# Layer 1 of a gated recurrence: when GpSimd adds x, and where VectorE's additions of sums stand

## The chip, the cores and the metric

The kernel runs on one core of a Trainium2 chip, in one launch. The time is device microseconds of that core. TensorE does the matrix products into PSUM banks, ScalarE (ACT) the sigmoids, tanhs and copies into PSUM, VectorE (DVE) and GpSimd (POOL) the elementwise work, SyncE (SP) starts the transfers. Each engine takes its instructions in the program's order and waits on semaphores for the others. In the profile PEld is TensorE's loading of weights, which runs beside its products.

## The reference

Two recurrent layers of width 512 over 64 sequences of 128 steps, with a residual after each, all in float32:

```python
x = x + L0(x, cond)          # gates by sigmoid, normalised; cumulative products and sums over time
vz, vr, vh = cond @ C_z + b_z, cond @ C_r + b_r, cond @ C + b
xz, xr, xh = x @ W_z, x @ W_r, x @ W
def step(h, (xzt, xrt, xht)):
    z  = sigmoid(xzt + h @ U_z + vz)
    r  = sigmoid(xrt + h @ U_r + vr)
    hh = tanh(xht + (r * h) @ U + vh)
    h  = (1 - z) * h + z * hh
    return h, h
out = x + scan(step, 0, ...)
```

Layer 1 (the `step` above) is a chain of 128 steps: h of a step is needed for the gates of the next.

## The kernel before

Layer 0 runs until about 690 us, in 16 groups of 4 sequences. It is not touched.

Layer 1 splits the 64 sequences into two streams of 32. A step of one stream follows a step of the other, so that one stream's elementwise work can run under the other's products. In the text a *half step* is one step of one stream, about 4.5 us from its first sigmoid to the next one's (of the other stream); two make the step of all sequences. In the code, `halves` makes it in two parts, with a `yield` between them.

What a half step issues, with its lines:

- TensorE: the products of h with U_r and U_z (`g<-w_s,h`, L464), then one or two products for later steps, then those of r*h with U (`g<-w_s,fi`, L464), then again one or two products for later steps (L602).
- ScalarE: r (L918), z (L927), tanh (L957), and copies of the share of x and cond of a coming step into the gates' bank (`put_share`, L871).
- VectorE: r*h (L922) and its transpose (L923), each in two halves of 64 columns; in the second part z*hh (L969), the new h (L970) and its transpose (L974).
- GpSimd: 1-z (L933) and (1-z)*h (L934).
- The output: GpSimd adds x to the transposed h (L985, into `hh`), VectorE transposes that back into the output tile (L994), and SP stores four steps at a time (L1028). The call of L994 waits in a list, `deferred`, and is made in the first part of the next half step, after the reads.

The products for later steps are x @ W of all three gates for 8 steps of all sequences at once. They are made by two nested levels of a scheme with 7 products instead of 8 (classes and functions `Outer`, `products`, `sum_tasks`, `place`). It needs sums of blocks of x before the products (GpSimd, L810, drawn by `take_sums`) and sums of blocks of the result after them. For the latter the program keeps lists:

- `to_read`: results in PSUM banks. `read(n)` takes up to n of them: VectorE adds a result to a block in SBUF (`W<-r,W`, L704), for some of them first a common part (L699). A bank can be written again only when it has been read; `free` reads on until it has. So the position of a read on VectorE sets when a product (or a copy by ScalarE, L615) that uses the bank again can start.
- `to_add_c`: additions of two SBUF blocks on VectorE (`W<-W`, L719); `add_c()` takes one. `to_add`: the same on GpSimd (L724).
- `to_store`: finished blocks, stored by SP to DRAM (L732) at the start of the next half step; a step loads its share from there (L865).

In a half step of the program before, the order of the calls around the change is: in the first part, r*h (L922, L923), z, L933 and L934, shared parts, `add(1)` (L724), `take_sums` (L810), products, `read(reads[0] and ...)`, `deferred` (L994); in the second part the products of r*h, tanh, L969, L970, L974, then L985, `add_c()` (L719) and `read(reads[1])`. `reads` is (4, 1) or (4, 0) for most steps and (2, 2) where a stream takes two steps in a row. The last 7 steps of each stream (`apart`, from step 121) split the gates differently and have no L985.

The order on each engine is pinned as the program issues it (`pin`); transfers are placed around it.

Of the kernel before, what the change touches and what calls it, by code (L numbers as in the profile page):

```python
# [12 lines left out]
ALU = mybir.AluOpType  # L13
# [6 lines left out]
def kernel(  # L20
# [38 lines left out]
    nc = tc.nc  # L59
# [11 lines left out]
    SB = B // 2  # L71
# [7 lines left out]
    def pin(instruction):  # L79
        return tc.keep_in_program_order(instruction)  # L80
# [199 lines left out]
    def chunk_products(g, c, between=None):  # L280

        f, i = fs[c % 2], is_[c % 2]
        fb, ib = by_batch(f), by_batch(i)
        p = gate(g, c, 0)
        pin(nc.scalar.activation(fb, p, AF.Sigmoid, bias=biasT[:, 0, c : c + 1]))
        if g == 0 and c == 0:
            w0_transposed(0, 2)
        elif g == 0 and c + 1 < K:
            w0_transposed(c + 1, 0)
        if between:  # L290
            between()
        p = gate(g, c, 1)
        pin(nc.scalar.activation(ib, p, AF.Sigmoid, bias=biasT[:, 0, K + c : K + c + 1]))
        if g == 0 and c == 0:
            transposed(condT, cond_sb, n=B)
            w0_transposed(1, 0)
        elif g == 0 and c + 1 < K:
            w0_transposed(c + 1, 1)
        if g + 1 < NG:
            for u, m in ((), ((0, 0), (0, 1)), ((1, 0),), ((1, 1),))[c]:  # L300
                x_joined(g + 1, u, m)
        p = gate(g, c, 2)
        if g == 0 and c + 1 < K:
            for n in range(1 if c == 0 else 2, 3):
                w0_transposed(c + 1, n)
        return p
# [135 lines left out]
    def conditioning():  # L442

        vs = []
        for s in range(2):
            p = psum.tile([P, 3, P], F32, tag="tp", name=f"pv{s}")
            matmuls(p, lambda k: condT[:, k, s * SB : (s + 1) * SB], [cw[:, k] for k in range(K)])
            whole = const.tile([P, 3, P], F32, name=f"whole_v{s}")
            pin(nc.vector.tensor_tensor(whole, p, bias1, ALU.add))
            vs.append(whole)  # L450
        return vs
# [106 lines left out]
    def x_of(st, t):  # L558

        return x4[t // TH][:, :, t % TH, st.batches]  # L560
# [4 lines left out]
    class Outer:  # L565
# [121 lines left out]
        def read(self, block, common):  # L687


            (m, j), n, r = block, self.n, self.bank(block)  # L690

            while n in (0, 5) and (m, j) in waiting:
                add(1)
            while n == 5 and (m, j) in waiting_c:
                add_c()
            if j == 1 and not common:
                if not hasattr(self, "common"):
                    shared_to_copy[0]()
                pin(nc.vector.tensor_tensor(r, r, self.common, ALU.add))  # L699
                return  # L700
            u, s5, c = (acc[:, i, m, j] for i in range(3))
            v1, v21 = v_x[:, j], v_x[:, 2 + j]
            dst, other = ((u, v1), (c, u), (u, u), (s5, v21), (c, s5), (u, u), (c, u))[n]
            pin(nc.vector.tensor_tensor(dst, r, other, ALU.add))  # L704
            unread.discard(r.name)
            if n == 1:
                self.store(c, 0, m, j)
            elif n == 4:
                waiting_c.add((m, j))
                to_add_c.append(lambda: self.add_c(c, u, m, j))  # L710
            elif n == 5:
                waiting.add((m, j))
                to_add.append(lambda: self.add(s5, u, m, j))
            elif n == 6:
                self.store(c, 1, m, j)

        def add_c(self, c, u, m, j):
            waiting_c.remove((m, j))
            pin(nc.vector.tensor_tensor(c, c, u, ALU.add))  # L719
            self.store(c, 0, m, 2 + j)  # L720

        def add(self, s5, u, m, j):
            waiting.remove((m, j))
            pin(nc.gpsimd.tensor_tensor(s5, s5, u, ALU.add))  # L724
            self.store(s5, 1, m, 2 + j)
# [13 lines left out]
    to_copy, shared_to_copy = [], []  # L739
    to_read, unread = [], set()  # L740
    to_add, waiting = [], set()
    to_add_c, waiting_c = [], set()
# [10 lines left out]
    sums_to_take, taken = [], set()  # L753
# [12 lines left out]
    def sum_tasks(group):  # L766
# [24 lines left out]
        def halves(d):  # L791
            *ts, op = d
            return [(*[t[:, k] for t in ts], op) for k in range(HC)]

        outer = [
            [(base - 1, ("s", group, i, k), d_) for k, d_ in enumerate(halves(d))]
            for i, d in enumerate(wsums(x_[0][0], x_[0][1], x_[1][0], x_[1][1], s_))
        ]
# [6 lines left out]
    def take_sums(n):  # L805
        for m in range(n):
            if not sums_to_take or sums_to_take[0][0] > state["begun"]:
                return m
            _, name, a = sums_to_take.pop(0)
            pin(nc.gpsimd.tensor_tensor(*a))  # L810
            taken.add(name)
        return n

    ahead = []
# [21 lines left out]
    class Stream:  # L836
# [56 lines left out]
        def halves(self, t, filler=None, between=None, targets=lambda: (0, 0), busy=False, reads=(4, 0)):  # L893
# [40 lines left out]
                    pin(nc.gpsimd.tensor_tensor(r, r, h_, ALU.mult))  # L934
            while shared_to_copy:
                shared_to_copy[0]()
            add(1)
            take_sums(2 if busy else 3)
            place(targets()[0], busy)
            if filler:  # L940
                filler()
            read(reads[0] and max(reads[0], len(to_read) - 2))
            while deferred:
                deferred.pop(0)()
            if between:
# [3 lines left out]
            h, hT, hh = (tile_[:, n] for n in range(3))  # L949
# [31 lines left out]
            if apart:  # L981
                deferred.append(output)
                return
            pin(
                nc.gpsimd.tensor_tensor(  # L985
                    hh.rearrange("p (k b) -> p k b", b=SB),
                    hT.rearrange("p (k b) -> p k b", b=SB),
                    x_of(self, t),
                    ALU.add,
                )  # L990
            )

            def output():
                pin(nc.vector.transpose(o, hh))  # L994
                self.store(t)

            deferred.append(output)
            if APART <= t + AHEAD < S:

                pin(nc.gpsimd.tensor_copy(ident.rearrange("p (k b) -> p k b", b=SB), x_of(self, t + AHEAD)))  # L1000
                deferred.append(lambda: pin(nc.vector.transpose(self.output(t + AHEAD), ident)))
            add_c()
            read(reads[1])
            if t + 2 < S and not direct(self, t + 2) and all((t + 2, q) in stored for q in range(Q)):
                self.load_share(t + 2)
# [29 lines left out]
    APART, AHEAD = 121, 10  # L1035
    last_outputs = []
    deferred = []
    pending = []

    shares_d = [dram.tile([TW * B, Q, 3 * P], F32, name=f"shares{n}") for n in range(4)]  # L1040

    for g in range(NG):
        for c in range(K):
# [7 lines left out]
            if (g, c) == (1, 1):  # L1051
                vs = []
                p = chunk_products(g, c, between=lambda: vs.extend(conditioning()))
            else:
                p = chunk_products(g, c)
# [160 lines left out]
    for n in range(2):  # L1216
        t = work.tile([P, 5, 3, P], F32, tag="xt", bufs=2, name=f"w_inner{n}")
# [97 lines left out]
        n += len(steps)  # L1315
    while deferred:
        deferred.pop(0)()
    assert not ahead and not to_read and not to_copy and not shared_to_copy and not sums_to_take


# [32 lines left out]
```

## Time and profile before

| | |
|---|---|
| median of 3 runs | 1877.04 us (1876.59 to 1879.87) |
| the profiled execution | 1878.12 us, of which the span of its instructions is 1876.3 |
| mean clock granted to TensorE | 0.999 |
| from 785 to 1800 us: busy PE, PEld, DVE, ACT, POOL | 1014.25, 641.39, 770.97, 455.05, 587.34 of 1015.00 us |
| L922 (r*h) there | 438 times, mean 224 ns |
| L985 (adds x) there | 219 times, mean 497 ns; idle before it 194.6 us, 173.9 of them until L974 |
| L719 there | 53 times, mean 552 ns |
| L810 (sums before the products), 128x128 and 128x256 | 479 to 529 ns, 749 to 792 ns |
| L704 and L699 (reads) there | 539 to 543 ns, 555 ns |

The page names an engine's share of the span, then the chain of work that ended last, followed back from the end. In the timeline each row has a start in us from the span's start, a duration, the engine, the line, output and inputs, and in brackets how long the engine was idle and what ended it. The ends of matmuls are modelled, so the distance from one start to the next tells more of TensorE than the durations.

### The profile page before, as it was taken

Reading aid. Unit: us, or ns where it says so; the run is one execution under the profiler, and the core shown is the slowest. Engines: PE = TensorE matmul, PEld = TensorE weight load, DVE = VectorE, ACT = ScalarE, POOL = GpSimd, SP = SyncE. Lnnn points to the kernel's source line nnn. Section 1 sums busy time; section 2 is a strip of 40 time slices with the busy share of each in tenths; the row PEclk is TensorE's granted clock in tenths of the full one; section 3 lists DMA queues with packets and bytes.
Section 4 is the critical chain, followed back from the end, with each engine's and each line's share of the span. In section 5 each row is a group of like instructions: output and inputs, shape, how many; then the busy total and the mean of one; then the engine's idle time right before and its main releaser. Section 6 shows DMA issues by size and latency. Waiting matters only on the chain.

```text
span 1876.3 us, 62311 instructions
## 1 busy us (share of the span) xinstructions
PE 1864.2 (99%) x24793; PEld 1054.2 (56%) x24793; DVE 1504.9 (80%) x3438; ACT 722.6 (39%) x1888; POOL 865.1 (46%) x1544
## 2 busy tenths in 40 slices
PE   9999999999999999999999999999999999999998
PEld 5444444444444445566666666666666666666567
DVE  5899999999999976777777777777777777777786
ACT  3232223222232233344444444444444444444434
POOL 1233232333333344546556556466565565565650
PEclk9999999999999999999999999999999999999999
DMA  7765433444333241334334344344343343443343
GB/s 181 176 124 119 82 70 73 88 82 83 73 76 65 49 86 29 101 90 142 112 101 142 94 115 133 104 124 126 96 137 109 99 141 101 114 130 96 111 111 78
DMA packets 366754, 195.38 MB, mean 104 GB/s; under 512 B 225332, under 2 KB 352064, under 8 KB 366464
## 3 DMA queue, kind: packets, MB, share of 16 engines
q1 hardware_dynamic: 366280, 191.33, 40.9%
q8 instruction: 195, 3.19, 0.7%
q14 instruction: 95, 0.78, 0.1%
q10 hardware_dynamic: 184, 0.07, 0.0%
HBM read 78.63 MB, written 81.13 MB: 85 GB/s over the span
## 4 chain that ended last, share of the span: by engine, by line
PE 98%; DVE 1%; issue 0%; DMA 0%; ACT 0%; SPq 0%; DVEq 0%; ACTq 0%
PE g L464 36%; PE p L232 35%; PE r L602 14%; PE r12a L602 4%; PE shared L602 4%; PE r12b L602 4%; PE gz L464 1%; PE tp L190 0%; PE pv L464 0%; DMA x<-in_x_dram 0%; DVE W L704 0%; PE g_first L464 0%; DVE fi L923 0%; DVE fi L922 0%; DVE r L339 0%
## 5 line engine op out<-in xcount | busy, mean ns | idle before, releaser
L232 PE MATMUL p<-xT,W 128*128 128x512 f32 (+1 forms) x1560 | 661.9, 586 | 0.0
L232 PEld LDWEIGHTS p<-xT,W 128*128 128x128 f32 x1560 | 293.5, 190 | 361.6 <-issue 359.1
L464 PE MATMUL g<-w_s,h 128*32 128x256 f32 (+1 forms) x8128 | 481.0, 373 | 2.3 <-issue 1.6
L464 PEld LDWEIGHTS g<-w_s,h 128*32 128x32 f32 x8128 | 301.4, 110 | 179.4 <-issue 83.2
L464 PEld LDWEIGHTS g<-w_s,fi 128*32 128x32 f32 x8128 | 222.7, 109 | 113.9 <-issue 55.4
L464 PE MATMUL g<-w_s,fi 128*32 128x128 f32 x8128 | 276.3, 273 | 2.7 <-DVE fi L922 1.3
L922 DVE TENSOR_TENSOR fi<-fi,h 128x64 f32<-128x64 f32 (+1 forms) x494 | 112.3, 227 | 179.3 <-ACT fi L918 178.5
L985 POOL TENSOR_TENSOR h<-h,x 128x128 f32<-128x128 f32 x242 | 121.3, 501 | 232.4 <-DVE h L974 206.8
L314 POOL COPY first<-condT 128x4 f32<-128x4 f32 x64 | 12.6, 196 | 461.8 <-DVE h L386 432.8
L918 ACT ACTIVATE fi<-g 128x128 f32<-128x128 f32 x254 | 70.6, 278 | 327.7 <-PE g L464 308.9
L933 POOL TENSOR_SCALAR fi<-fi 128x128 f32<-128x128 f32 x240 | 72.6, 302 | 236.6 <-DVE fi L922 226.5
L704 DVE TENSOR_TENSOR W<-r,W 128x384 f32<-128x384 f32 x315 | 169.2, 539 | 7.4
L310 ACT ACTIVATE fi<-fi 128x512 f32<-128x512 f32 x64 | 40.4, 631 | 340.6 <-DVE fi L351 340.6
L957 ACT ACTIVATE h<-g 128x128 f32<-128x128 f32 x255 | 70.9, 278 | 236.2 <-PE g L464 236.2
L923 DVE STREAM_TRANSPOSE fi<-fi 128x64 f32<-128x64 f32 (+1 forms) x494 | 122.2, 247 | 22.8 <-PE r12a L602 0.5
L969 DVE TENSOR_TENSOR h<-h,fi 128x128 f32<-128x128 f32 (+1 forms) x264 | 94.9, 359 | 43.8 <-ACT h L957 43.1
L253 POOL TENSOR_TENSOR x<-xT,h 128x512 f32<-128x512 f32 x63 | 122.6, 1946 | 4.9
L934 POOL TENSOR_TENSOR fi<-fi,h 128x128 f32<-128x128 f32 x240 | 110.8, 462 | 20.0
L970 DVE TENSOR_TENSOR h<-h,fi 128x128 f32<-128x128 f32 (+1 forms) x264 | 97.7, 370 | 27.2 <-POOL held L810 0.9
L810 POOL TENSOR_TENSOR held<-held 128x128 f32<-128x128 f32 x240 | 113.7, 488 | 3.1
L602 PE MATMUL r<-w_inner,held 128*32 128x384 f32 x1080 | 114.6, 486 | 0.0
L339 DVE RECIPROCAL r<-r 128x256 f32<-128x256 f32 x60 | 104.2, 1737 | 0.0
(158 smaller groups left out, 2721.5 us busy)
## 6 DMA issues: line engine op xcount, KB each, us to landing
shares<-W SPq DMA_DIRECT2D x240, 192.0 KB, 2.1
xz<-shares SPq DMA_DIRECT2D x480, 48.0 KB, 1.9
whole_v<-shares SPq DMA_DIRECT2D x480, 48.0 KB, 2.0
x2d<-x SPq DMA_DIRECT2D x63, 256.0 KB, 4.2
words<-held SPq DMA_DIRECT2D x240, 64.0 KB, 2.1
out_dram<-o SPq DMA_DIRECT2D x240, 64.0 KB, 1.8
xw_None<-x2d SPq DMA_DIRECT2D x56, 256.0 KB, 3.4
w_rows<-in_L_cond_W_f_dram SPq DMA_DIRECT2D x4, 256.0 KB, 5.7
```

The costliest lines, as they stand in the source:

```text
L232: nc.tensor.matmul(p[:, tokens], lhsT=W0[:, c, n, k, :], rhs=xT[g][:, k, tokens], start=(k == 0), stop=(k == K - 1),)
L253: nc.gpsimd.tensor_tensor(x2.rearrange("p (t b) -> p t b", b=GB)[:, ts], xT[g][:, c, :].rearrange(f"{layout(g)} -> p t b", b=GB)[:, ts], b ...
L339: pin(nc.vector.reciprocal(r, r))
L464: nc.tensor.matmul(p[q * SB : (q + 1) * SB], lhsT=lhsT(k), rhs=part(wk, q), start=(start and k == 0), stop=(stop and k == len(w) - 1), ski ...
L602: nc.tensor.matmul(self.bank(bank)[q * SB : (q + 1) * SB], lhsT=a[:, q * SB : (q + 1) * SB], rhs=w_, start=start, stop=True, skip_group_ch ...
L704: pin(nc.vector.tensor_tensor(dst, r, other, ALU.add))
L810: pin(nc.gpsimd.tensor_tensor(*a))
L922: pin(nc.vector.tensor_tensor(rh[:, e], r[:, e], h_[:, e], ALU.mult))
L923: pin(nc.vector.transpose(rhT[:, e], rh[:, e]))
L934: pin(nc.gpsimd.tensor_tensor(r, r, h_, ALU.mult))
L970: pin(nc.vector.tensor_tensor(h[:, e], hh[:, e], r[:, e], ALU.add))
L985: nc.gpsimd.tensor_tensor(hh.rearrange("p (k b) -> p k b", b=SB), hT.rearrange("p (k b) -> p k b", b=SB), x_of(self, t), ALU.add,)
```

## The change

The addition of x (L985) is no longer issued at the end of a half step's second part. It goes to a new list, `unsummed`, which the first part of the next half step empties: after that step's L933 and L934, and before `add(1)` and the sums. The output's transpose is put into `deferred` at that point, so it still comes in the same first part as before, behind the reads. `add_c()` is no longer called at the end of the second part; it is called in the first part, ahead of the reads, and when it has something to add, the number of reads to take is less by one (unless more than that are waiting beyond two).

```diff
@@ in halves, first part
             while shared_to_copy:
                 shared_to_copy[0]()
+            while unsummed:
+                unsummed.pop(0)()
             add(1)
             take_sums(2 if busy else 3)
             place(targets()[0], busy)
             if filler:
                 filler()
-            read(reads[0] and max(reads[0], len(to_read) - 2))
+            added = len(to_add_c[:1])
+            add_c()
+            read(reads[0] and max(reads[0] - added, len(to_read) - 2))
             while deferred:
                 deferred.pop(0)()
@@ in halves, second part
-            pin(
-                nc.gpsimd.tensor_tensor(
-                    hh.rearrange("p (k b) -> p k b", b=SB),
-                    hT.rearrange("p (k b) -> p k b", b=SB),
-                    x_of(self, t),
-                    ALU.add,
-                )
-            )
 
             def output():
                 pin(nc.vector.transpose(o, hh))
                 self.store(t)
 
-            deferred.append(output)
+            def summed():
+                pin(
+                    nc.gpsimd.tensor_tensor(
+                        hh.rearrange("p (k b) -> p k b", b=SB),
+                        hT.rearrange("p (k b) -> p k b", b=SB),
+                        x_of(self, t),
+                        ALU.add,
+                    )
+                )
+                deferred.append(output)
+
+            unsummed.append(summed)
             if APART <= t + AHEAD < S:
 
                 pin(nc.gpsimd.tensor_copy(ident.rearrange("p (k b) -> p k b", b=SB), x_of(self, t + AHEAD)))
                 deferred.append(lambda: pin(nc.vector.transpose(self.output(t + AHEAD), ident)))
-            add_c()
             read(reads[1])
```

What is computed stays the same.

More of the change, by code (lines that the diff above doesn't have):

```diff
@@ L1037 @@
     deferred = []
+    unsummed = []
     pending = []
@@ L1317 @@
         deferred.pop(0)()
-    assert not ahead and not to_read and not to_copy and not shared_to_copy and not sums_to_take
+    assert not ahead and not to_read and not to_copy and not shared_to_copy and not sums_to_take and not unsummed
 _INS = [
```

## The prediction

> **What bounds the kernel now.** I read the page (busy times, chain of waits), then the timeline of layer 1 half step by half step, then the order of the instructions before and after. The page first:
>
> ```profile
> span 1876.3 us, 62311 instructions
> PE 1864.2 (99%) x24793; PEld 1054.2 (56%) x24793; DVE 1504.9 (80%) x3438; ACT 722.6 (39%) x1888; POOL 865.1 (46%) x1544
> PE 98%; DVE 1%; issue 0%; DMA 0%; ACT 0%; SPq 0%; DVEq 0%; ACTq 0%
> ```
>
> TensorE is full, and the chain that ended last lies on it for 98%. The change adds and removes no matmul, so it can only move what makes TensorE wait in layer 1 (from about 690 us). The busy rows do not show those waits, because the matmuls' ends are modelled; I read them from the starts. Undisturbed, in the timeline around 1404 us, the two products before `fi` start at 1403.85 and 1404.49, `fi` at 1405.14: 0.645 us each. At 1155 us:
>
> ```profile
> 1154.46 0.84 PE L602 MATMUL r<-w_x,x 128*32 128x384 f32 x8
> 1154.47 0.31 DVE L974 STREAM_TRANSPOSE h<-h 128x128 f32<-128x128 f32 x1
> 1154.72 0.28 ACT L918 ACTIVATE fi<-g 128x128 f32<-128x128 f32 x1 [1.58 <-PE g L464]
> 1155.00 0.45 POOL L985 TENSOR_TENSOR h<-h,x 128x128 f32<-128x128 f32 x1
> 1155.03 0.50 DVE L922 TENSOR_TENSOR fi<-fi,h 128x64 f32<-128x64 f32 x1 [0.24 <-ACT fi L918]
> 1155.11 0.84 PE L602 MATMUL shared<-w_inner,held 128*32 128x384 f32 x8
> 1155.57 0.24 DVE L923 STREAM_TRANSPOSE fi<-fi 128x64 f32<-128x64 f32 x1
> 1155.73 0.18 DVE L922 TENSOR_TENSOR fi<-fi,h 128x64 f32<-128x64 f32 x1
> 1155.96 1.08 PE L464 MATMUL g<-w_s,fi 128*32 128x128 f32 x32
> ```
>
> The last product starts at 1155.11, `fi` at 1155.96: 0.85 instead of 0.645, 0.20 us lost. L985 on GpSimd covers 1155.00 to 1155.45; L922, 0.18 to 0.23 elsewhere, takes 0.50 and ends 0.08 after L985. So L922 stands still while L985 runs, and r*h reaches TensorE late. I went through all starts from 785 to 1800 us this way. All losses together are 8.1 us; those over 0.06 us fall into five kinds:
>
> - A: L985 alone lies over L922: 19 places, 2.63 us.
> - B: L969 and L970 stood behind GpSimd's sums L810, so L974 is late, then L922 (as at 863.35): 9 places, 1.89.
> - C: L719 stands at the end of the half step, then L985 comes over L922: 4 places, 0.86 (and 0.40 and 0.21 after 1800).
> - D: a product waits for a read (L704) of its bank: 2 places of 0.46 (1142.99 and 1563.65).
> - E: one of 0.28 at 1415, where the second L923 starts late.
>
> What L719 costs in the middle of a half step is also there, at 920 us:
>
> ```profile
> 919.94 0.46 POOL L934 TENSOR_TENSOR fi<-fi,h 128x128 f32<-128x128 f32 x1
> 920.12 0.70 DVE L719 TENSOR_TENSOR W<-W 128x384 f32<-128x384 f32 x1
> 920.36 0.77 POOL L810 TENSOR_TENSOR held<-x,held 128x128 f32<-128x128 f32 x1
> ```
>
> L719 (0.52 alone) waits for L934's end at 920.40 and ends 0.42 later, at 920.82; the L810 behind it takes 0.77 instead of 0.46 and ends 0.31 after L719. A VectorE addition of two SBUF tiles and a GpSimd operation take turns; reads from PSUM (L704, L699: 0.52 to 0.56) and transposes are not held up.
>
> **The change part by part.** Times below run from the start of a half step's first sigmoid (L918). Undisturbed: L922 at 0.31, last L923 done at 1.20, GpSimd's L933 1.08 to 1.38, L934 1.47 to 1.93, then a slot each 0.42; the next sigmoid at 4.54 (4.47 in some). A late L922 costs TensorE its lateness less about 0.06: 0.27 late cost 0.20, 0.19 cost 0.11.
>
> *L985 behind L934.* 242 additions of 0.46 us move from just after L974 (from 3.6 to 4.5) to 1.88 to 2.34. There VectorE mostly does reads, which do not collide, and no matmul waits for an output. So kind A goes: -2.63. The transpose L994 now waits for L985's end at 2.34. With two reads or more in front VectorE isn't there earlier (1.20+2x0.5); with one read it waits 0.7 us, and L969 behind it starts at 2.6 rather than at tanh's end, 2.4: 0.2 us on a chain whose result TensorE needs a step of the other stream later. Cost 0. The output's copy to DRAM goes later by at most this; nothing waits for it.
>
> *The sums L810 one slot later.* L985 takes the first slot, so each sum comes 0.42 later. Products that wait for a sum start 1.46 us or more after it in 420 of 421 cases, 0.20 after it once (1198.5): 0, at most +0.3. In kind B the slots are filled as before with other work (L985 where the first operation stood), so L969 and L970 meet the same ends and L974 is as late: 0 taken, -0.5 at best (second L922, 0.37 there under L985, back to 0.18). GpSimd's queue as a whole loses its wait for L974 and ends earlier than before.
>
> *L719 in the middle.* The new order of instructions keeps TensorE's and ScalarE's exactly. On VectorE 46 of 60 L719 move from behind L974 to just behind the last L923 of the next half step, and one read there goes to a later half step. 46 half steps then have one L719 in the middle and 6 have two. That removes kind C: -0.86, and -0.61 after 1800. The price: L719 stands behind L933, which ends at 1.38; with the 0.41 above it ends at 1.79; then L704 to 2.16, L699 to 2.75, L704 to 3.22 (start to start 0.45, 0.59, 0.47), L994 0.23, L969 at 3.45, L970 at 3.80, L974 done at 4.44. L922 is late only if L974 ends after 4.93 (it started 0.08 before L974's end). Margin 0.49: 0 taken for the half steps with one L719. Upper bound in the slower rival.
>
> With two L719: the second one starts at 2.16, L985 then runs to 2.57 (L934 ends at 2.11 after the first), L719 done at 2.98, 699 to 3.49, 704 to 3.96, L969 4.19, L974 done at 5.18; L922 0.25 late, 0.19 lost. Six times: +1.1 (0 if L719 gets ahead of L933 and L985, +3 at 0.5 each).
>
> The Trainium skill, "GPSIMD Engine Reference", section Key points, says that GpSimd shares its SBUF interfaces with VectorE and contends with VectorE instructions that have two SBUF inputs. By that rule this half of the change is a loss by itself, since it puts such an instruction where a PSUM read stood, next to GpSimd's busiest stretch; by the rule alone each of the 46 would be charged, at the measured 0.70-0.52, 8.3 us on VectorE. The rows agree that the collision is there, but VectorE's 0.49 margin takes it.
>
> *Reads later.* Pairing each bank's last read with the next write to it, one place gets worse: the product at 1142.99 waits for the second L704 of its half step (1141.92 to 1142.94), and L719 comes in front of both: 0.5 later, +0.5 (bounds 0.4 and 0.7). The one at 1563.65 stays. ScalarE's copies onto banks keep 0.59 us or more but for three with 0.11; one of these gets L719 in front, 0.6 late, which delays a tanh that has a step's cover: 0, at most +0.3. SP's queue gets its stores and loads of shares in another order; a store that comes a half step later can push the load behind it. Store and load land in 2.1 and 1.9 us, 4.0 together, less than the 4.54 of a half step, and put_share's copies (L871) wait 0.2 us for a share in all today: 0, at most +1.
>
> *After 1800.* Half steps are 3.89 there, so the limit for L974 is 4.28. Two of them get L719, three reads and L1001 (0.23): L974 done at 4.67, 0.33 lost, and 0.27 where GpSimd's tail differs: +0.6, against the -0.61 of kind C.
>
> Sum: -2.63 -0.86 -0.61 +1.1 +0.5 +0.6 = **-1.9 us**. The profiled execution took 1878.12 (span 1876.3 and 1.8 around it); it would go to 1876.2. The median shown is 1877.04, 1.1 below it, so **1875.1**.
>
> Bounds: the best that is on the table is all losses from 785 to 1800 plus kind C after it, 8.1+0.6, without any price. Taking away the E and D that nothing here touches, 1.2, and half of the crumbs below 0.06, 0.7, leaves 6.8: 1870.2.
>
> **The rivals.**
>
> *Everything that collides goes, the prices do not come.* For: GpSimd's work is now one piece from L933 on, with a free second before the next L922; if L719 gets in front of L933 the double ones cost nothing, and part of B may go with the smoother queue. Against: B's slots. -2.63-0.86-0.61-1.89+0.5 = -5.5: 1871.5.
>
> *Slower: L974 late behind the shifted sums.* One mechanism: in the half steps with L719 in the middle, VectorE comes to L969 and L970 at 3.5 to 3.8, where the third sum or L724's successors now run, since all of GpSimd is 0.42 (and 0.3 for the collision with L719) later. The full lock costs L969 0.59 (0.84 at 861.50 against 0.25) and L970 0.35 (0.63 against 0.29): L974 done at 5.38, 0.39 lost. 31 of the half steps with L719 have three sums or L724 behind L985. It decides from about ten such places on; with 15 it is +5.9: 1881. Against: by the slots above the third sum ends at 3.8, so L969 alone meets it, which the margin covers.
>
> *L985 only changes its victim.* It runs into L719 and pushes the sums into L969; gains and prices cancel: 1877. It lies in the forecast's range and class.
>
> **How the numbers follow.** A measurement of this kernel can tell about 0.2% (3.75 us) from no change. Forecast with the last rival, 0.50, its own range 1873.4 to 1878; everything goes, 0.31; slower, 0.19. Range 1870.4 to 1879.4: it takes in the fast rival and stops short of the slow one's centre. Faster by over 0.2% needs below 1873.3: 0.33. Slower needs above 1880.8: 0.17. Within: 0.50.
>
> **What would show it.** Right: L922's mean over 785 to 1800 (0.224) falls to about 0.20, since no first L922 lies under L985; L985 no longer waits for L974 (173.9 us) but follows L934; `fi` starts 0.645 after the last product at 1155 and 1062; still 0.2 at the places of kind B, about 1 us at the place of 1142.99. L719's mean rises from 0.55 to 0.6 or more. Wrong: new losses at `fi` in half steps with one L719, with L974 ending after the next sigmoid has ended; or TensorE waiting for a sum or a share.

## The result, and the profile after

The changed kernel takes 1881.42 us (median of 16 runs, 1879.68 to 1885.03), the kernel before 1877.39 us beside it (16 runs, 1876.59 to 1880.59). The ratio is 1.0021, with a 95% interval of 1.0014 to 1.0028: 4 us slower, where 1.9 us faster was forecast, and outside the range that was given.

Line numbers up to 934 are the same in both kernels. Behind that, what was L957, L969, L970, L974 and L994 is L961, L973, L974, L978 and L991 in the changed kernel; the addition of x, L985 before, is L996. In the text the old numbers are used, and the new ones only beside rows of the trace. From the page of the changed kernel:

```profile
span 1879.6 us, 61968 instructions
PE 1865.6 (99%) x24793; PEld 1064.4 (57%) x24793; DVE 1529.3 (81%) x3438; ACT 722.2 (38%) x1888; POOL 861.0 (46%) x1544
PE 96%; DVE 2%; issue 1%; ACT 1%; POOL 1%; DMA 0%; ACTq 0%; DVEq 0%; POOLq 0%
L933 POOL TENSOR_SCALAR fi<-fi 128x128 f32<-128x128 f32 x240 | 91.9, 383 | 469.1 <-DVE fi L922 392.3
L996 POOL TENSOR_TENSOR h<-h,x 128x128 f32<-128x128 f32 x242 | 111.7, 462 | 3.1 <-DVE h L978 3.1
```

The span is 3.3 us longer. In the chain of waits VectorE's share goes from 1 to 2%, and GpSimd now appears with 1%. L996 hardly waits for the transpose of h any more: 3.1 us of idle time in the whole span, against 173.9 us before in 785 to 1800 us alone. The idle time has not gone, though: it stands in front of L933, which waits for L922.

No L922 lies under the addition of x any more, and at 16 of the 23 places where one did the loss is gone, as forecast (at four a sum now stands in its stead, at three VectorE comes late behind two L719). From the timeline at 1062 us, one of the 16: the sigmoid, the first L922, the last product before `fi`, and `fi`:

```profile
1061.56 0.28 ACT L918 ACTIVATE fi<-g 128x128 f32<-128x128 f32 x1 [0.56 <-PE g L464]
...
1061.87 0.22 DVE L922 TENSOR_TENSOR fi<-fi,h 128x64 f32<-128x64 f32 x1 [0.55 <-ACT fi L918]
1061.94 0.86 PE L602 MATMUL r12b<-w_inner,held 128*32 128x384 f32 x8
...
1062.58 0.97 PE L464 MATMUL g<-w_s,fi 128*32 128x128 f32 x28
```

L922 takes 0.22, and `fi` starts 0.64 after the product. But at 1155 us, the place that the prediction shows, the loss stays:

```profile
1154.94 1.47 POOL L810 TENSOR_TENSOR held<-x 128x256 f32<-128x256 f32 x2
...
1155.72 0.28 ACT L918 ACTIVATE fi<-g 128x128 f32<-128x128 f32 x1 [1.63 <-PE g L464]
...
1156.03 0.46 DVE L922 TENSOR_TENSOR fi<-fi,h 128x64 f32<-128x64 f32 x1 [0.56 <-ACT fi L918]
1156.05 0.86 PE L602 MATMUL shared<-w_inner,held 128*32 128x384 f32 x8
...
1156.91 0.43 PE L464 MATMUL g<-w_s,fi 128*32 128x128 f32 x8
```

Two sums L810 run until 1156.41, 0.69 after the sigmoid's start. L922 ends 0.08 after that, and `fi` starts 0.86 after the product: 0.22 is lost, as before (0.20). L985 had stood there; now the sums that it pushed back stand there. And the half step behind a full one, which had lost nothing, loses too. The two kernels in the same half step, first the kernel before: the sigmoid, GpSimd and VectorE in its timeline at 867 us:

```profile
867.52 0.28 ACT L918 ACTIVATE fi<-g 128x128 f32<-128x128 f32 x1 [1.20 <-PE g L464]
...
867.51 0.46 POOL L810 TENSOR_TENSOR held<-x 128x128 f32<-128x128 f32 x1
867.93 0.45 POOL L985 TENSOR_TENSOR h<-h,x 128x128 f32<-128x128 f32 x1
...
867.83 0.23 DVE L922 TENSOR_TENSOR fi<-fi,h 128x64 f32<-128x64 f32 x1 [0.52 <-ACT fi L918]
```

and the same rows of the changed kernel:

```profile
867.63 0.28 ACT L918 ACTIVATE fi<-g 128x128 f32<-128x128 f32 x1 [1.25 <-issue]
...
867.86 0.46 POOL L810 TENSOR_TENSOR held<-x 128x128 f32<-128x128 f32 x1
...
867.94 0.46 DVE L922 TENSOR_TENSOR fi<-fi,h 128x64 f32<-128x64 f32 x1 [0.29 <-ACT fi L918]
```

Before, the third sum ends at 867.97, L922 finishes at 868.06, and L985 comes behind it. In the changed kernel the same sum begins 0.35 later, 0.08 ahead of L922 instead of 0.32, and L922 waits for all of it. GpSimd's queue ends earlier than before, 0.69 after the sigmoid's start instead of 0.86; but what stands at its end is now running when L922 wants to start, where L985 had come in behind it.

To count this, I took every start of TensorE from 785 to 1800 us and sorted the losses above 0.055 us by what stood over the first L922, or ahead of it on VectorE (number of places, us lost):

| | before | after |
|---|---|---|
| L922 under the addition of x | 23: 3.49 | 0 |
| L922 under a sum L810 alone or with an ident copy | 0 | 28: 6.13 |
| VectorE late at L922 (behind L970, L974) | 9: 1.89 | 6: 0.53 |
| a product waits for a read | 2: 0.92 | 2: 1.36 |
| a product waits for a sum | 0 | 1: 0.31 |
| second half of r*h late | 2: 0.34 | 0 |
| L922 on time after its sigmoid, nothing over it | 0 | 20: 1.79 |
| all the small ones | 1.41 | 0.31 |
| sum | 8.06 | 10.42 |

After 1800 us the losses go from 8.24 to 8.84. Together that is 3.0 of the 3.3 us of span.

### The profile page after: what moved, and what is told of

It reads as the page before. It is cut to its first block, busy times and chain, and to the rows that moved or that the text cites. A ratio compares the mean times of both kernels' runs of the same rounds, so it can differ in the third digit from the quotient of the medians.

```text
span 1879.6 us, 61968 instructions
## 1 busy us (share of the span) xinstructions
PE 1865.6 (99%) x24793; PEld 1064.4 (57%) x24793; DVE 1529.3 (81%) x3438; ACT 722.2 (38%) x1888; POOL 861.0 (46%) x1544
## 4 chain that ended last, share of the span: by engine, by line
PE 96%; DVE 2%; issue 1%; ACT 1%; POOL 1%; DMA 0%; ACTq 0%; DVEq 0%; POOLq 0%
PE g L464 36%; PE p L232 35%; PE r L602 14%; PE shared L602 4%; PE r12a L602 3%; PE r12b L602 3%; PE gz L464 1%; PE tp L190 1%; DVE fi L922 0%; DVE fi L923 0%; PE pv L464 0%; ACT fi L918 0%; DVE W L704 0%; POOL held L810 0%; PE g_first L464 0%
## 5 line engine op out<-in xcount | busy, mean ns | idle before, releaser
L464 PEld LDWEIGHTS g<-w_s,h 128*32 128x32 f32 x8128 | 310.5, 110 | 170.8 <-issue 79.3
L933 POOL TENSOR_SCALAR fi<-fi 128x128 f32<-128x128 f32 x240 | 91.9, 383 | 469.1 <-DVE fi L922 392.3
L922 DVE TENSOR_TENSOR fi<-fi,h 128x64 f32<-128x64 f32 (+1 forms) x494 | 108.2, 219 | 169.1 <-ACT fi L918 168.4
L918 ACT ACTIVATE fi<-g 128x128 f32<-128x128 f32 x254 | 70.4, 277 | 333.4 <-PE g L464 230.5
L961 ACT ACTIVATE h<-g 128x128 f32<-128x128 f32 x255 | 70.7, 277 | 231.8 <-PE g L464 231.8
L974 DVE TENSOR_TENSOR h<-h,fi 128x128 f32<-128x128 f32 (+1 forms) x264 | 113.0, 428 | 9.1
L934 POOL TENSOR_TENSOR fi<-fi,h 128x128 f32<-128x128 f32 x240 | 110.8, 462 | 20.0
L996 POOL TENSOR_TENSOR h<-h,x 128x128 f32<-128x128 f32 x242 | 111.7, 462 | 3.1 <-DVE h L978 3.1
L810 POOL TENSOR_TENSOR held<-held 128x128 f32<-128x128 f32 x240 | 111.5, 479 | 3.1
L991 DVE STREAM_TRANSPOSE o<-h 128x128 f32<-128x128 f32 x240 | 73.0, 304 | 46.8 <-POOL h L996 43.9
L973 DVE TENSOR_TENSOR h<-h,fi 128x128 f32<-128x128 f32 (+1 forms) x264 | 103.6, 393 | 6.7 <-ACT h L961 6.5
```

The lines of the kernel that those rows point to most:

```text
L464: nc.tensor.matmul(p[q * SB : (q + 1) * SB], lhsT=lhsT(k), rhs=part(wk, q), start=(start and k == 0), stop=(stop and k == len(w) - 1), ski ...
L922: pin(nc.vector.tensor_tensor(rh[:, e], r[:, e], h_[:, e], ALU.mult))
L973: pin(nc.vector.tensor_tensor(hh[:, e], hh[:, e], z[:, e], ALU.mult))
L974: pin(nc.vector.tensor_tensor(h[:, e], hh[:, e], r[:, e], ALU.add))
L996: nc.gpsimd.tensor_tensor(hh.rearrange("p (k b) -> p k b", b=SB), hT.rearrange("p (k b) -> p k b", b=SB), x_of(self, t), ALU.add,)
```

## The experiments

Beside each time stands the ratio to the kernel before, run on the same chip. "200 half steps" is the time from the 21st to the 221st start of `fi` in the profiled execution; it takes 924.82 us in the kernel before and 927.15 in the changed one, and holds nothing of layer 0. Without its losses it is 917.3 us in both (924.82-7.53 and 927.15-9.85). The one kernel that was run twice (the fastest one below) gives 919.35 and 919.40. The counts of L922 are those of 785 to 1800 us, sorted as above.

### The two halves of the change, each by itself

The move of L985 alone (against the changed kernel):

```diff
-            added = len(to_add_c[:1])
-            add_c()
-            read(reads[0] and max(reads[0] - added, len(to_read) - 2))
+            read(reads[0] and max(reads[0], len(to_read) - 2))
...
+            add_c()
             read(reads[1])
```

> Only the addition of x (L985) is moved behind L934 of the next half step; L719 stays at the end of a half step and no read is dropped. Reading of the changed kernel's trace (theory 1): the move itself brings two new losses. (a) GpSimd's sums L810 come a slot of 0.42 us later and the last of them lies over the next half step's L922, about 0.2 us at each of some 15 places. (b) the sigmoid L918 gets a wait for GpSimd (L934 of the step before) in nearly all half steps and starts 0.32 us instead of 0.26 after the last product of h, so that a late L922 has no slack left. Theory 1: the gains of kind A and C (-3.5) are eaten here, 1877 to 1879.5; L918 starts 0.32 after. Theory 2 (the loss comes from L719 in the middle and from the dropped reads): the gains stand, 1873.5 to 1874.5.

Measured: 1879.38 us, ratio 1.0007 (0.9998 to 1.0016); 200 half steps 925.57. L922 under the addition of x: none, under L810: 22 places, 5.04 us. The move frees 3.49 us there and 0.80 where VectorE was late (1.89 to 1.09), and pays 5.04 for them; the row "L922 on time after its sigmoid" has 21 places, 1.24 us. The interval of the ratio still takes in no change; the 200 half steps are 0.75 longer. The gains that theory 2 expected did not come.

The move of L719 alone (against the kernel before):

```diff
-            read(reads[0] and max(reads[0], len(to_read) - 2))
+            added = len(to_add_c[:1])
+            add_c()
+            read(reads[0] and max(reads[0] - added, len(to_read) - 2))
...
-            add_c()
             read(reads[1])
```

> Only the additions L719 go to the middle of a half step in place of a read; L985 stays at the end. Theory 1 (the loss is in the move of L985): kind C goes (-0.9 to -1.5), the read at 1143 costs +0.5, half steps with two L719 +0.6, so 1877 to 1878.5, and L918 starts 0.26 us after the last product of h in most half steps, as before. Theory 2 (the loss is L719 in the middle): 1880 or more.

Measured: 1880.39 us, ratio 1.0012 (1.0003 to 1.0021); 200 half steps 927.10. So theory 1 alone falls too. This half loses clear of noise, the other by its 200 half steps only; their times over the kernel before, 0.07 and 0.12%, add up to about the 0.21% of the whole. Why this half loses stands in its timeline at 1220 us, GpSimd's rows:

```profile
1220.26 0.72 POOL L933 TENSOR_SCALAR fi<-fi 128x128 f32<-128x128 f32 x1 [0.63 <-DVE fi L922]
1221.06 0.46 POOL L934 TENSOR_TENSOR fi<-fi,h 128x128 f32<-128x128 f32 x1
1221.47 1.01 POOL L724 TENSOR_TENSOR W<-W 128x384 f32<-128x384 f32 x1
...
1223.86 0.45 POOL L987 TENSOR_TENSOR h<-h,x 128x128 f32<-128x128 f32 x1
```

and VectorE's:

```profile
1220.30 0.52 DVE L719 TENSOR_TENSOR W<-W 128x384 f32<-128x384 f32 x1
...
1223.95 0.45 DVE L922 TENSOR_TENSOR fi<-fi,h 128x64 f32<-128x64 f32 x1 [0.51 <-ACT fi L918]
```

L719 runs its 0.52 undisturbed and L933, 0.30 elsewhere, takes 0.72. All of GpSimd's half step comes 0.42 later, and the addition of x (L987 here), last in its queue, lies over the next L922. There are 31 such places (4.90 us) instead of 23 (3.49). VectorE is late at 12 (2.45) instead of 9 (1.89), and the read at 1143 costs 0.93 instead of 0.46.

Whether it is the place of L719 or the dropped read was tried with the two next ones. L719 behind the reads:

```diff
             added = len(to_add_c[:1])
-            add_c()
             read(reads[0] and max(reads[0] - added, len(to_read) - 2))
+            add_c()
```

> The run with the move of L719 alone (1880.39), but with L719 behind the reads of the half step instead of in front of them; one read less is still taken. If that run's loss comes from L719 holding up L933 (0.72 us instead of 0.30, all of GpSimd 0.4 later, L985 over the next L922 in 26 half steps, not 18): L933's mean falls from about 0.38 back to 0.30, the 1.4 us go, the read at 1143 is 0.46 again (-0.5), and the time is 1877.5 to 1879. If the dropped read or L974 coming late is the cause: 1880 or more, with more places where VectorE comes late to L922.

Measured: 1878.02 us, ratio 0.9998 (0.9989 to 1.0007); 200 half steps 924.42. The group of L933 from 785 to 1800 us (count, busy time, mean ns, idle time before it):

```profile
L933 POOL TENSOR_SCALAR fi<-fi 128x128 f32<-128x128 f32 x219 | 65.8, 301 | 204.0 <-DVE fi L922 193.5 <-ACT r L615 4.8 <-DVE fi L923 2.5
```

Its mean is 301 ns again (381 with L719 ahead of the reads), L922 lies under the addition of x at 27 places, but for 3.40 us only, and the read at 1143 costs 0.45 again. This half of the change costs nothing if L719 stands elsewhere in the same half step.

L719 ahead of the reads and no read dropped:

```diff
-            added = len(to_add_c[:1])
             add_c()
-            read(reads[0] and max(reads[0] - added, len(to_read) - 2))
+            read(reads[0] and max(reads[0], len(to_read) - 2))
```

> The run with the move of L719 alone (1880.39), with L719 ahead of the reads as there, but no read dropped for it. If L719 holding up L933 is the cause: 1880 to 1881.5, L922 under L985 at some 26 places as there. If the dropped reads are the cause: 1877.5 to 1879.

Measured: 1881.79 us, ratio 1.0017 (1.0008 to 1.0026); 200 half steps 927.71. The time is where the first theory has it (0.3 above), but the places are not: 20 under the addition of x (3.02 us), and VectorE late at 19 (4.78) instead of 12 (2.45). The additional read fills VectorE. By these counts the dropped read is no cost, but keeps some of VectorE's margin; the ratios of the two runs, 1.0017 and 1.0012, do not tell them apart.

### Which of GpSimd's operations comes last

L985 behind the sums, its transpose a half step later (against the changed kernel):

```diff
-            while unsummed:
-                unsummed.pop(0)()
             add(1)
...
             while deferred:
                 deferred.pop(0)()
+            while unsummed:
+                unsummed.pop(0)()
```

> The changed kernel, with L985 behind the sums of its half step instead of in front of them, and its transpose a half step later. The sums keep the slots of the kernel before, and L918 has a wait for GpSimd in only 46 of 254 cases. Theory 1 (sums later, sigmoid's wait): the second losses of each pair (868.82, 942.66 and the like, about 3) and the three of 0.26 go, those of the read at 1143 and of two L719 stay: 1875 to 1877.5. Theory 2 (L719 in the middle): 1880 or more. If L985 lies over the next L922 where GpSimd is full (L724 and three sums), those places keep 0.2 each, and it ends at 1878 to 1879.

Measured: 1879.07 us, ratio 1.0006 (0.9997 to 1.0015); 200 half steps 925.28. L922 lies under the addition of x at 19 places, at 10 of them under a sum as well, for 4.07 us. The third case of the expectation is the one: the losses of each pair (two half steps in a row, as at 864 and 868) stay, only the operation in them changes. With VectorE late (2.59) they make 6.66 us, as much as the changed kernel loses in these two rows (6.13+0.53); that the sums agree to the hundredth is chance, for their parts differ. Where GpSimd has L724 and three sums its half step is too long, and whatever is last lies over L922. What this order gains lies elsewhere: the row of 1.79 is gone (see the sigmoid's wait below), and after 1800 us 7.36 is lost instead of 8.84.

### Opening GpSimd's window

In both kernels L933 starts 1.08 us after the sigmoid in most half steps and never earlier, because it writes 1-z over r, which L922 must have read; when GpSimd's queue has run out it stands idle until then. With 1-z and (1-z)*h in the new h's tile (on top of the changed kernel; the tile is only taken earlier):

```diff
             h_, hT_, g = self.h, self.hT, self.g
+            tile_ = work.tile([P, 3, P], F32, tag="h", bufs=4, name=f"h{self.s}_{t}")
+            h, hT, hh = (tile_[:, n] for n in range(3))
...
                 else:
+                    r = h
                     pin(nc.gpsimd.tensor_scalar(r, z, -1.0, 1.0, ALU.mult, ALU.add))
                     pin(nc.gpsimd.tensor_tensor(r, r, h_, ALU.mult))
...
-            tile_ = work.tile([P, 3, P], F32, tag="h", bufs=4, name=f"h{self.s}_{t}")
-            h, hT, hh = (tile_[:, n] for n in range(3))
```

> The changed kernel, with 1-z and (1-z)*h written into the new h's tile and not over r. L918 then needs no wait for GpSimd (in no half step), the tanh takes one. L933 no longer has to wait for L922 to have read r, so GpSimd may start half a us earlier and meet the second L922. If the sigmoid's added wait is a main cause: each late L922 costs 0.06 less (some 30 places, -1.8) and the three losses of 0.26 at 1132, 1587 and 1703 go (-0.8): 1878 to 1879.5, L918 0.26 after the last product. If it is not: 1881 to 1882. If L933 and L934 over the second L922 make the second half of r*h late: slower than 1883.

Measured: 1874.27 us, ratio 0.9980 (0.9971 to 0.9989); 200 half steps 921.34. It is faster than any case of the expectation, which counted on the sigmoid and not on the window. No first L922 is held up by GpSimd any more; 2.77 us are left where VectorE is late, 1.75 of them at three half steps with two L719 (0.58, 0.59 and 0.58), and 1.34 at the two reads.

The same tile in the kernel before, with nothing of the change:

> The kernel before, with nothing of the change, but with 1-z and (1-z)*h in the new h's tile: L933 no longer waits for L922 to have read r, and GpSimd begins a half step some 0.55 us earlier (L933 at 0.54 after the sigmoid instead of 1.08, as the run of the changed kernel with this tile showed). Theory W (what the half step loses is GpSimd's window: it begins at 1.08, and with L724 and three sums its last operation lies over the next L922, whatever that operation is): the places of kind B and the pairs go, kind A stays where L985 waits for L974 and lies over L922 (-2 to -4): 1874 to 1876. If the early start helps only together with the change: 1877 to 1879.

Measured: 1876.25 us, ratio 0.9992 (0.9983 to 1.0001); 200 half steps 923.07. The medians are 1.5 us apart, 0.25 above the first case, and the interval takes in no change; the 200 half steps are 1.75 shorter. L985 behind L974 still lies over L922 at 22 places, 3.73 us.

And the tile with the move of L985 alone, L719 left at the end of a half step:

> The own tile with the move of L985 alone; L719 at the end of a half step, no read dropped. Theory W: with the window open the move of L985 pays what was predicted of it (kind A, -2.6), and the price of L719 in the middle (the read at 1143 0.4 more, three places of 0.58 with two L719) is saved against the changed kernel with this tile (1874.27): 1871 to 1873. If L719 in the middle is needed for the gain: 1875 or more.

Measured: 1871.59 us, ratio 0.9967 (0.9955 to 0.9979); 200 half steps 919.35. A second time:

> The kernel of 1871.59 once more, beside the run with the window shut: 1870.5 to 1872.5 if its gain over the kernel before is real.

Measured: 1872.26 us, ratio 0.9970 (0.9957 to 0.9982). This version beats both kernels: 5.4 to 6.2 us less than the kernel before. Neither part does it alone: the move of L985 without the tile took 1.5 us more than the kernel before, the tile without the move 1.5 us less, neither clear of noise. Its timeline at the same product as at 1155 above (L920 is the sigmoid, L924 r*h, L936 and L937 what were L933 and L934):

```profile
1151.11 0.77 POOL L810 TENSOR_TENSOR held<-x 128x256 f32<-128x256 f32 x1
...
1151.78 0.28 ACT L920 ACTIVATE fi<-g 128x128 f32<-128x128 f32 x1 [1.52 <-PE g L464]
...
1152.09 0.23 DVE L924 TENSOR_TENSOR fi<-fi,h 128x64 f32<-128x64 f32 x1 [0.44 <-ACT fi L920]
1152.16 0.84 PE L602 MATMUL shared<-w_inner,held 128*32 128x384 f32 x8
...
1152.31 0.30 POOL L936 TENSOR_SCALAR h<-fi 128x128 f32<-128x128 f32 x1 [0.42 <-ACT fi L929]
...
1152.51 0.18 DVE L924 TENSOR_TENSOR fi<-fi,h 128x64 f32<-128x64 f32 x1
...
1152.69 0.46 POOL L937 TENSOR_TENSOR h<-h,h 128x128 f32<-128x128 f32 x1
...
1152.81 0.42 PE L464 MATMUL g<-w_s,fi 128*32 128x128 f32 x8
```

L936 follows z at 0.53 after the sigmoid's start. The last sum ends at 1151.88, 0.10 after it and not 0.69, so L924 is free, and `fi` starts 0.65 after the product. Of 785 to 1800 us only 2.64 us of losses are left.

### Is it the window, or the sigmoid's wait?

The own tile also changes something else. In the changed kernel the sigmoid L918 has a wait for GpSimd (L934 of its stream's step before) in 223 of 254 cases, in the kernel before in 51, with the own tile in none. With that wait it starts 0.32 us after the start of the product that follows the products of h, without it 0.26. It is not the number of engines: in the kernel before, from 785 to 1800 us, 90 sigmoids that wait for VectorE besides TensorE start at 0.26, like the 85 that wait for TensorE alone, and 44 that wait for GpSimd besides TensorE at 0.32. In the trace the 90 carry TensorE's wait, which ends last, themselves, with VectorE's in a semaphore instruction ahead of them; the 44 carry GpSimd's, with TensorE's ahead. Whether that order is what costs the 0.06 was not tried. Two tests of the two causes. First, the fast version (the tile and the move of L985) with the window shut again, and the sigmoid still free of the wait:

```diff
                     r = h
+                    pin(nc.gpsimd.tensor_copy(r[:, :1], rh[:, P - 1 :]))
                     pin(nc.gpsimd.tensor_scalar(r, z, -1.0, 1.0, ALU.mult, ALU.add))
```

> The kernel of 1871.59 (own tile, L985 behind L934, L719 at the end), with one more instruction on GpSimd ahead of L933: a copy of one column (128x1) of the second half of r*h into the new h's tile, which L933 then overwrites. GpSimd so again begins only when L922 is done (L933 at 1.1 to 1.2 after the sigmoid, not 0.54), while the sigmoid still has no wait for GpSimd. Theory W (the window decides): L922 lies under L810 again at some 20 to 30 places, 4.5 to 6.5 us in 785 to 1800, and the time goes back to 1877 to 1880. If the gain came from the sigmoid's wait being gone: it stays at 1871 to 1873.

Measured: 1882.16 us, ratio 1.0024 (1.0014 to 1.0034); 200 half steps 927.72. From its timeline (L936 is the added copy, L937 what was L933; the releaser named in this row is a product, but 356.5 of the 362.7 us that L936 waits from 785 to 1800 us are put down to r*h, L924):

```profile
1160.95 0.18 POOL L936 COPY h<-fi 128x1 f32<-128x1 f32 x1 [0.60 <-PE r L602]
1161.23 0.30 POOL L937 TENSOR_SCALAR h<-fi 128x128 f32<-128x128 f32 x1
```

L922 lies under L810 at 19 places again (6.04 us), VectorE is late at 7 (2.51). All of the gain is gone, and 2 us more than expected; the copy itself makes GpSimd's start later still: L937 begins 0.41 after the second r*h has ended (1160.82), in the changed kernel 0.17. The run does not part the later start from the copy's own time on GpSimd: L937 starts 1.33 after the sigmoid, where L933 started at 1.08. But with no sigmoid waiting for GpSimd the time is not below the changed kernel's, so the sigmoid's wait is not what the tile gains by; GpSimd's earlier start is.

Second, the kernel before with the sigmoid's wait added, and a control:

```diff
+            if t and not apart:
+                pin(nc.vector.tensor_copy(rh[:, :1], r[:, :1]))
             for n in range(1 + apart) if t else ():
```

> The kernel before, with a copy of one column (128x1) on VectorE ahead of L969 that reads GpSimd's (1-z)*h. It takes over L970's wait for GpSimd, and the sigmoid L918 then has a wait for GpSimd of its own in 237 of 254 cases, like the changed kernel (223), not in 51. Together with the next run, whose copy reads z instead and leaves the 51: if the sigmoid's added wait costs 0.06 us wherever L922 is late, this one is 1 to 2.5 us slower than the next, and L918 starts 0.32 us after the last product of h, not 0.26. If the wait is free: no difference.

> The kernel before, with the same copy of one column, which reads z: L918's waits stay as before (51 of 254). The copy itself is some 0.1 us of VectorE in each half step ahead of L969: 1877.5 to 1879.5. Control for the run with the copy of (1-z)*h; the two differ only in what the column is read from.

The control reads `z[:, :1]` in the same place. Measured, the wait first and the control second: 1880.02 us, ratio 1.0010 (1.0001 to 1.0019), and 1878.68 us, ratio 1.0006 (0.9998 to 1.0015). L918 starts at 0.32 and 0.26 in them, as expected. The run with the wait has 17 places of 0.06 (0.99 us in all) at which L922 is on time after its sigmoid and nothing lies over it, and the control has none; the changed kernel has 17 of the same size, most of them at the same products. So the wait does cost, but not where the expectation had it: a late L922 is set by the end of GpSimd's operation, and a sigmoid 0.06 later changes nothing there. The control loses 0.72 us more where VectorE is late (2.99 against 2.27; four of these places, 0.28 each, lie under the addition of x as well), so that 200 half steps take 926.16 and 926.12 us, and the intervals overlap. About 1 us gross is what the rows show; a net cost is not shown. At the three other places of the changed kernel's row (1132, 1587 and 1703 us, 0.26 each) L918 starts 0.60 after that product; what holds it there was not found.

## Why the prediction was wrong, point by point

- *Kinds A and C go, -3.49 in 785 to 1800.* Right as far as L985 goes: 23 places and 3.49 us, now none. In seven of these half steps another loss stands in its place (1.13 us before, 1.23 after).
- *The sums L810 one slot later: 0, at most +0.3.* This is the step that failed. I looked at who waits for a sum (the product at 1199.61 does, 0.31, my bound) and at L969 and L970, and not at whether the last sum now reaches the next L922. It does, at 28 places, for 6.13 us. The move alone showed it without any L719: 22 places, 5.04 us. The other six (1152 and the like) come with L719 in the middle: there the last sum ends 0.60 after the sigmoid's start, and 0.20 in the run with the move alone.
- *Kind B unchanged, since the slots are filled as before.* The loss stayed (0.21 at 864.07, 937.92 and so on), but for another reason: L974 comes nearly in time there (L922 starts at 0.35 after the sigmoid instead of 0.63), and L922 lies under a sum.
- *GpSimd's queue as a whole ends earlier.* Right, and it does not help. From 785 to 1800 us GpSimd is still at work 0.31 after the sigmoid, when L922 would start, in 89 half steps before and in 30 after. But before, an L985 came in behind L922 in 24 of the 89, as at 867; at the 28 places it is a sum that began ahead of L922 and ends 0.60 to 0.69 after the sigmoid's start.
- *L719 stands behind L933; L974 has 0.49 of margin.* The margin held for the half steps with one L719: the six places with VectorE late are those behind two L719 in one half step, as forecast, and cost 0.53 together, not 1.1. But the order was wrong. L719 goes first and L933 takes 0.72, so the delay goes to GpSimd's full queue, not to VectorE. In my sum this half came to +0.7 (-0.86-0.61+1.1+0.5+0.6), in the run with L719 alone to 2.5 by the medians (1880.39-1877.89): the delay of GpSimd was not in it. With L719 behind the reads that loss is gone.
- *The forced read, +0.5.* Right: 0.94 at 1143.74, where the kernel before lost 0.46. At 1565.01 it is 0.42, before 0.46: right as well.
- *L994 waits for L985, cost 0.* Right: 43.9 us of idle time on VectorE, and no loss.
- *After 1800: -0.61+0.6, together nothing.* Measured +0.60; it was not taken apart.
- *L922's mean 0.20, L719's 0.6 or more.* 0.216 and 0.537: the first not low enough, the second wrong, both for the reasons above.
- The slower rival had the right time, 1881, and the wrong place. It put the loss at L974 behind the shifted sums; VectorE late at L922 fell from 1.89 to 0.53 us. The mechanism that decided, the sums over the next L922, was in none of my cases; the last rival came nearest, with the sums pushed into L969. That 1881 came out of another loss is chance.

The Trainium skill, "SBUF — State Buffer", section "Who interferes with whom", says that a VectorE instruction with two SBUF inputs contends with a GpSimd instruction that reads SBUF, and that the issue order decides who blocks. The rows at 867 agree: the L810 that starts 0.08 ahead of L922 makes it wait to its end. The rows at 1220 do not agree if the recorded start is taken as the issue: L933 starts 0.04 ahead of L719, and it is L933 that is held. Whether the recorded start is the issue, no run here shows.

## What to carry to other kernels

Where an engine's queue is full in some of the stages, moving one operation in it does not free the next critical operation; look for what ends last in the queue, whichever it is, and compare that end with the critical start, stage by stage. Then look for why the queue starts late: here a result written over its input made L933 start at 1.08 us after the sigmoid instead of 0.53. Another place for the result was worth little by itself (1.5 us, not clear of noise), but with it the move of L985, a loss or nothing before, paid 4.7 us (1876.25 to 1871.59). Price both sides of a contention before you say who waits.

## What had not been expected of the hardware

- GpSimd's L933, with one input, is held by VectorE's L719 (0.72 instead of 0.30 us), though it was recorded as started 0.04 earlier. Beside the 0.18 of r*h in the fast version the same operation takes its 0.30, and delays nothing; their rows overlap by 0.10 there, no more than L922's 0.18 overlaps a sum whose end it has waited for (it ends 0.08 after).
- A wait for GpSimd makes the sigmoid start 0.06 us later even when GpSimd has long been done: 0.32 and not 0.26 after the product. A wait for VectorE does not. The extra wait appears where VectorE has already waited for GpSimd elsewhere, so that the new h no longer carries the wait for (1-z)*h itself: the copy of (1-z)*h brought it to 237 of 254 sigmoids, the copy of z left it at 51.
